# Own rows copied by ScalarE and fetched rows added by the gathering DMA, in a sparse graph kernel on one core

## The chip, the cores and the metric

The kernel runs on 1 core of one Trainium2 chip. The core has TensorE (PE, matrix products), VectorE (DVE), ScalarE (ACT), GpSimd (POOL) and SyncE (SP); each runs its own instructions in their order and waits for the others by semaphores. Data moves between HBM and the core's SBUF by 16 DMA engines. They are fed by queues: SP and ACT issue plain transfers (queues q1 and q10 in the profile), POOL issues transfers whose rows are named by an index list (q0). Time is device time from start to end of the one launch, in microseconds (us). The figure is the median of the runs; the profile is one more execution, with every instruction recorded.

## What is computed

The input is `x` of 32 matrices (512 nodes by 256 features) and one adjacency matrix `adj` of 512 x 512, about 1.6% of it and the diagonal not zero. Four graph layers follow each other. Layers 0 and 3 are the ones that matter here:

```python
pre_u = einsum('bud,dk->buk', h, W1[:d])
pre_v = einsum('bvd,dk->bvk', h, W1[d:])
hidden = relu(pre_u[:, :, None, :] + pre_v[:, None, :, :] + b1)
S = sigmoid(einsum('buvk,ko->buvo', hidden, W2)[..., 0] + b2[0])
a = einsum('buv,bud->bvd', S * A_a, h)
m = einsum('uv,bud->bvd', A_m, h) * h
z = beta1*h + beta2*(a @ Wa + ba) + beta3*(m @ Wm + bm)
```

For every pair of nodes (u, v) a row of 256 sums goes through a relu and is multiplied with `W2` and summed. `S` is multiplied with `adj`, so only pairs that `adj` holds count: these are the edges. Layer 1 is `z + relu(adj @ z @ W.T + b)`; layer 2 is an attention with a softmax over rows of 512.

## The kernel before

The kernel counts the nonzero entries at run time and takes a sparse path (`sparse_path`) when they fit, as they do here; the dense path is only compiled. In the sparse path, the 32 matrices go in 8 groups of 4 (`NB = 4`). For each group there are these streams of work, each a generator that yields after every piece:

- `first` loads `x`, turns it and computes `pre_u` and `pre_v` for all nodes (`pre`, lines 565 to 588). They are written by queue SP to a table in HBM with two rows of 1024 numbers per node: the even row holds `pre_u + b1` of the 4 matrices, the odd row `pre_v`.
- `edges` (lines 616 to 724), once for layer 0 and once for layer 3: the edge stage, which the change is in.
- `middle`: rest of layer 0, layers 1 and 2, and `pre` of layer 3. It starts by loading the matrix of `S * adj` (`load`, L732).
- `last`: the rest of layer 3.

An edge stage works through 36 items (`ITEMS`) of 128 edges each. An item has a tile `mine` [128 x 1024] with the `pre_u` rows of its 128 own nodes, and a tile `rows` [128 x 1024] with the `pre_v` rows of their neighbours. For 32 items the own nodes are a block of 128 consecutive nodes: `mine` is loaded by queue SP (L652) once for a block and used by 8 items. The last four items of the list are panels of left-over edges with own nodes of their own: there `mine` is gathered by POOL (L655). `rows` is gathered by POOL (`fetch`, L662, issuing at L612). There are 5 buffers for `rows` and 3 for `mine`.

Per item, VectorE adds the two tiles in place (L691). Then there are two ways to the relu, the product with `W2` and the sum over 256 features for each of 4 matrices. On even items, and on the last three, VectorE does it in four instructions, one for each matrix, that give the sum too (L707, `accum_out`). On odd items VectorE does relu and product in one instruction over 1024 columns (L699), and ScalarE makes the four sums (L677), issued one item later (`summed`). After every fourth item the sigmoid follows in small instructions (`exp_of`, L597 on ScalarE; `sigmoid_of` and `run_1`, L601, L602 and L641 on VectorE). Each item's 128 x 4 results are scattered by POOL into a matrix in HBM (`put`, L606), one `put` per item, in POOL's order between the gathers. A gather is called 3 items ahead of its use (`LEAD`).

Two of the 16 edge stages are run with little beside them: layer 0 of the first group and layer 3 of the last. They get `spare` buffers (`rows_more`, 8 in all) and a lead of 5, and there all items go by L699 and L677.

The order of the work is set by `weave`: every piece of every stream has a planned time (in units of one group), and pieces are issued in order of these times. The layer 0 edge stage of a group is planned to end 0.04 to 0.06 of a group before its middle begins. A scheduler then lays the instructions on each engine. `behind(ins)` (L499) keeps an edge instruction on its engine behind the last-but-one piece of the middle stage. Before the change it is used for the add (L691), the sums (L677) and small instructions, and not for the gathers.

Of the kernel before, what the change touches and what calls it, by code (L numbers as in the profile page):

```python
# [12 lines left out]
ALU = mybir.AluOpType  # L13
# [22 lines left out]
ITEMS = NC * OWN + 2 * PANELS  # L36
# [382 lines left out]
class Sparse:  # L419
# [94 lines left out]
    def setup(self):  # L514


        for w in (self.m.g0, self.m.g3):
            self.nc.vector.tensor_scalar(w["nb2"], w["b2"], -1.0, None, ALU.mult)
        self.zero = self.act.tile([P, GROUP], F32, name="zero", tag="hWa3")
        self.nc.gpsimd.memset(self.zero, 0.0)  # L520

        edges = self.built = self.e.build(self.counts, self.adjT, self.lists, self.psum, self.big, self.act)
        for _ in range(NC):
            next(edges)
            yield
        self.rest = self.m.rest(self.big(F32, 2048), self.psum)
        next(self.rest)
        self.zeros(self.cells["0"])
        yield
        for _ in range(NC + 2 * (OWN // 2 + 1)):  # L530
            next(edges)
            yield
# [74 lines left out]
            out=g.cells[half], out_offset=bass.IndirectOffsetOnAxis(ap=at, axis=0), in_=s, in_offset=None  # L607
        )

    def fetch(self, rows, g, at):  # L610

        self.nc.gpsimd.indirect_dma_start(  # L612
            out=rows, out_offset=None, in_=g.table, in_offset=bass.IndirectOffsetOnAxis(ap=at, axis=0)
        )

    def edges(self, g, spare=()):

        nc, e, w = self.nc, self.e, g.w  # L620
        flat = "p c b -> p (c b)"
        own = g.self_s.rearrange(flat)
        ready, fetched = [], {}
        lead = LEAD_AT_ENDS if spare else LEAD
        tags = [None] * 5 + list(spare)
        mine = {}
        places = g.table.rearrange("(c p k) n -> c k p n", p=P, k=2)

        def own_1():
            self.sigmoid_of(own)  # L630
            diag = self.counts.diag.unsqueeze(2).to_broadcast([P, NC, NB])
            nc.vector.tensor_tensor(g.self_s, g.self_s, diag, ALU.mult)
            for q in range(2):
                diagonal = g.cells[q][q * HALF : q * HALF + HALF * (N + 1), :]
                diagonal = diagonal.rearrange("(c p a) b -> p c a b", p=P, a=N + 1)[:, :, 0, :]
                nc.sync.dma_start(diagonal, g.self_s[:, 2 * q : 2 * q + 2, :])

        def run_1(ks):
            self.sigmoid_of(g.s[:, ks, :].rearrange(flat))
            value = e.value[:, ks].unsqueeze(2).to_broadcast([P, ks.stop - ks.start, NB])  # L640
            nc.vector.tensor_tensor(g.s[:, ks, :], g.s[:, ks, :], value, ALU.mult)  # L641
            for k in range(ks.start, ks.stop):
                j = e.order[k]
                ready.append((e.half_of(j), e.cell[:, j : j + 1], g.s[:, k, :]))

        def fetch(n):
            j = e.order[n]
            c = j // OWN
            if c >= NC or c not in mine:
                t = self.gath.tile([P, GROUP], F32, name="mine", bufs=3)  # L650
                if c < NC:
                    nc.sync.dma_start(t, places[c, 0])  # L652
                    mine[c] = t
                else:
                    self.fetch(t, g, e.iu[:, j - NC * OWN : j - NC * OWN + 1])  # L655
            else:
                t = mine[c]
            if tag := tags[n % len(tags)]:
                rows = self.act.tile([P, GROUP], F32, name="rows_more", tag=tag)
            else:  # L660
                rows = self.gath.tile([P, GROUP], F32, name="rows")
            self.fetch(rows, g, e.iv[:, j : j + 1])  # L662
            fetched[n] = rows, t

        def put():

            at = next((n for n, r in enumerate(ready) if r[0] != self.half), 0)
            if ready:
                r = ready.pop(at)
                self.half = r[0]  # L670
                self.put(g, *r)

        def sums(k, rows):

            for b in range(NB):
                part = rows[:, b * D : (b + 1) * D]
                self.behind(nc.scalar.activation(part, part, AF.Identity, accum_out=g.s[:, k, b : b + 1]))  # L677

        summed = []
        self.half = 1  # L680
        for n in range(lead):
            fetch(n)
            yield

        todo = [(2, lambda: self.exp_of(w, own)), (4, own_1)]
        done = 0
        for k in range(ITEMS):
            for _ in range(2 if spare and len(ready) > 2 else 1):
                put()
            rows, other = fetched.pop(k)  # L690
            self.behind(nc.vector.tensor_tensor(rows, rows, other, ALU.add))  # L691
            if k + lead < ITEMS:
                fetch(k + lead)
            if summed:
                summed.pop(0)()
            if spare or k % 2 == 1 and k < ITEMS - 3:
                by_entry = rows.rearrange("p (b d) -> p b d", b=NB)
                w2 = w["W2bc"].unsqueeze(1).to_broadcast([P, NB, D])
                nc.vector.scalar_tensor_tensor(by_entry, by_entry, 0.0, w2, ALU.max, ALU.mult)  # L699
                summed.append(lambda k=k, rows=rows: sums(k, rows))  # L700
                if spare:
                    summed.pop(0)()
            else:
                for b in range(NB):
                    part = rows[:, b * D : (b + 1) * D]
                    at = g.s[:, k, b : b + 1]
                    nc.vector.scalar_tensor_tensor(part, part, 0.0, w["W2bc"], ALU.max, ALU.mult, accum_out=at)  # L707
            if k % 4 == 3 or k >= ITEMS - 3:
                ks = slice(done, k + 1)
                near = spare or k >= ITEMS - 5  # L710
                todo.append((k + (1 if near else 3), lambda ks=ks: self.exp_of(w, g.s[:, ks, :].rearrange(flat))))
                todo.append((k + (1 if near else 4), lambda ks=ks: run_1(ks)))
                done = k + 1
            while todo and todo[0][0] <= k:
                todo.pop(0)[1]()
            yield
        for _, f in todo:
            f()
        for _ in range(TAIL - 1):
            put()  # L720
            yield
        while ready:
            put()
        yield
# [643 lines left out]
```

## Time and profile before

| | us |
|---|---|
| median of 3 runs | 3111.6 (3107.93 to 3116.17) |
| span of the profiled execution | 3112.8 |
| TensorE busy | 2713.5 (87%) |
| VectorE busy | 2302.9 (74%) |
| GpSimd busy | 1531.2 (49%) |
| ScalarE busy | 1337.7 (43%) |
| 16 DMA engines, mean busy share | 68% |

The profiled execution's own time is its span; it lies 1.2 us over the median. A line of the profile's groups reads: line of the kernel, engine, operation, destination <- sources, sizes and count, then busy us and mean ns of one, then the engine's idle us just before these instructions and what ended most of that. A table of waits reads: who waited, at which line, for whom, then us in total, times, longest. In a table of windows each row is a stretch of the span; for each engine it has busy us and number of instructions, then the granted TensorE clock, the busy share of the DMA engines and GB/s. Some records of a trace are missing: the page counts 552 gathers into `rows` and 24 into `rows_more`, which make up the 576, but other groups can be a few short.

### The profile page before, as it was taken

The numbers are of one execution on the slowest core, as the hardware profiler recorded it, in microseconds if no ns is written. First come the engines' busy times: TensorE is split into PE (matmuls) and PEld (weight loads), VectorE is DVE, ScalarE is ACT, GpSimd is POOL, SyncE is SP. The second block draws the span as 40 slices with busy tenths as digits, with TensorE's granted clock in tenths as the row PEclk, the third lists the DMA queues.
The fourth block names the chain that finished last, engine by engine and source line by source line (L and its number), as shares of the span: only waits on it lengthen the run. The fifth ranks groups of instructions, "written<-read, shape, count | busy, mean of one in ns | idle before, by whom it ended". The sixth has DMA issues, their size and how long they took to land. (4 is left out here: it accounts for less than half of the span.)

```text
span 3112.8 us, 32475 instructions
## 1 busy us (share of the span) xinstructions
PE 2713.5 (87%) x8645; PEld 1639.7 (53%) x8646; DVE 2302.9 (74%) x6027; ACT 1337.7 (43%) x4101; POOL 1531.2 (49%) x1328
## 2 busy tenths in 40 slices
PE   6367878889998899989998899989998899879957
PEld 3133444446654566446654565545654466546636
DVE  6964877888689776988489785888679795772761
ACT  3553454444344433444354442544345343443440
POOL 2561553656345552656346562555436563450461
PEclk9688889999999999999999999999999999999979
DMA  8774657776778757776678766787578766551753
GB/s 278 267 238 151 210 164 242 248 261 214 225 214 293 220 189 227 245 263 216 210 212 258 236 196 211 243 266 234 177 225 273 247 220 200 182 183 49 231 196 115
DMA packets 302719, 679.40 MB, mean 218 GB/s; under 512 B 52672, under 2 KB 170944, under 8 KB 294336
## 3 DMA queue, kind: packets, MB, share of 16 engines
q0 software_dynamic: 122688, 414.40, 42.6%
q1 hardware_dynamic: 160880, 225.62, 22.0%
q10 hardware_dynamic: 18960, 37.24, 3.2%
q8 instruction: 70, 1.15, 0.1%
q14 instruction: 121, 0.99, 0.1%
HBM read 531.12 MB, written 146.01 MB: 218 GB/s over the span
## 5 line engine op out<-in xcount | busy, mean ns | idle before, releaser
L606 POOL DMA_INDIRECT cells<-s,cell x576 | 686.4, 1192 | 747.0 <-DMA cells<-s,cell 388.5
L612 POOL DMA_INDIRECT rows<-table,iv x552 | 667.6, 1209 | 619.9 <-DMA table<-puv 150.5
L691 DVE TENSOR_TENSOR rows<-rows,mine 128x1024 f32<-128x1024 f32 x552 | 667.4, 1217 | 191.7 <-DMA rows<-table,iv 173.3
L677 ACT ACTIVATE rows<-rows 128x256 f32<-128x256 f32 x1088 | 439.8, 407 | 506.6 <-DVE rows L699 477.3
L45 PE MATMUL pst<-adj,h 128*128 128x512 f32 x1024 | 452.6, 594 | 0.3 <-PE pst L946 0.3
L707 DVE SCALAR_TENSOR_TENSOR rows<-rows,L_gnn_W2bc 128x256 f32<-128x256 f32 x1120 | 415.0, 417 | 1.8
L45 PE MATMUL pst<-L_gnn_Wa,hT 128*128 128x256 f32 x1024 | 261.3, 406 | 104.8 <-DMA hT<-xT 56.2
L699 DVE SCALAR_TENSOR_TENSOR rows<-rows,L_gnn_W2bc 128x1024 f32<-128x1024 f32 x272 | 329.7, 1214 | 0.3
L45 PEld LDWEIGHTS pst<-adj,h 128*128 128x128 f32 x1024 | 193.4, 191 | 223.3 <-issue 219.4
L45 PEld LDWEIGHTS pst<-L_gnn_Wa,hT 128*128 128x128 f32 x1024 | 204.8, 205 | 151.8 <-issue 85.1
L45 PE MATMUL pst<-eT,feats 128*128 128x512 f32 x512 | 230.9, 604 | 13.0 <-ACT eT L958 13.0
L866 PE MATMUL pst<-WT,hT 128*128 128x256 f32 x512 | 155.1, 470 | 96.0 <-DVE hT L853 96.0
L45 PE MATMUL pst<-adjT,zW 128*128 128x512 f32 x512 | 227.7, 597 | 3.8 <-ACT zW L870 3.8
L1006 PEld LDWEIGHTS pst<-hWa,SA 128*128 128x128 f32 x896 | 213.8, 328 | 7.7 <-issue 4.1
L1006 PE MATMUL pst<-hWa,SA 128*128 128x256 f32 x896 | 216.8, 398 | 0.0
L814 ACT COPY flat<-SA 128x512 f32<-128x512 f32 x128 | 137.7, 1127 | 165.9 <-PE pst L45 83.7
L677 ACT ACTIVATION_READ_ACCUMULATOR rows<-rows 128x1 f32 x1088 | 205.4, 189 | 0.0
L845 PE MATMUL pst<-flat,hWa 128*128 128x512 f32 x448 | 196.8, 592 | 0.0
L866 PEld LDWEIGHTS pst<-WT,hT 128*128 128x128 f32 x512 | 121.4, 242 | 136.6 <-DVE hT L853 107.1
L579 DVE TENSOR_TENSOR puv<-pst,bc_L_gnn_b 128x256 f32<-128x256 f32 x256 | 104.4, 414 | 95.8 <-DMA table<-puv 58.6
L580 ACT COPY puv<-pst 128x256 f32<-128x256 f32 x256 | 93.5, 370 | 180.6 <-DVE puv L579 162.7
L45 PEld LDWEIGHTS pst<-eT,feats 128*128 128x128 f32 x512 | 97.2, 193 | 127.5 <-issue 109.4
(172 smaller groups left out, 3984.4 us busy)
## 6 DMA issues: line engine op xcount, KB each, us to landing
table<-puv SPq DMA_DIRECT2D x256, 256.0 KB, 5.7
SA<-cells POOLq DMA_DIRECT2D x64, 1024.0 KB, 7.2
h<-in_x_dram SPq DMA_DIRECT2D x64, 512.0 KB, 6.5
mine<-table SPq DMA_DIRECT2D x64, 512.0 KB, 5.5
hT<-xT SPq DMA_DIRECT2D x36, 512.0 KB, 5.0
h<-x2s SPq DMA_DIRECT2D x36, 512.0 KB, 4.4
xT<-hT ACTq DMA_DIRECT2D x32, 512.0 KB, 6.1
x2T<-yT SPq DMA_DIRECT2D x32, 512.0 KB, 5.5
```

What stands on the lines that cost most here:

```text
L45: nc.tensor.matmul(out, lhsT, rhs, start=(n == 0), stop=(n == len(pairs) - 1))
L579: nc.vector.tensor_tensor(puv[:, 0, :], pp[:, 0:D], w["b1bc"], ALU.add)
L606: self.nc.gpsimd.indirect_dma_start(out=g.cells[half], out_offset=bass.IndirectOffsetOnAxis(ap=at, axis=0), in_=s, in_offset=None)
L612: self.nc.gpsimd.indirect_dma_start(out=rows, out_offset=None, in_=g.table, in_offset=bass.IndirectOffsetOnAxis(ap=at, axis=0))
L677: self.behind(nc.scalar.activation(part, part, AF.Identity, accum_out=g.s[:, k, b : b + 1]))
L691: self.behind(nc.vector.tensor_tensor(rows, rows, other, ALU.add))
L699: nc.vector.scalar_tensor_tensor(by_entry, by_entry, 0.0, w2, ALU.max, ALU.mult)
L707: nc.vector.scalar_tensor_tensor(part, part, 0.0, w["W2bc"], ALU.max, ALU.mult, accum_out=at)
L814: self.nc.scalar.copy(flat[:, r, :], SA[r][:, :, b])
L845: nc.tensor.matmul(pz, hWa[:, r, cs], flat[:, r, :], start=(r == 0), stop=False)
L866: nc.tensor.matmul(pw[:, at], zT[:, d, cs], m.WT_1[:, d, :], start=(d + k == 0), stop=(d * k == 1))
L1006: nc.tensor.matmul(pz[:, k * D : (k + 1) * D], SA[r][:, cs, b], hWa[:, r, :], start=(r + k == 0), stop=False)
```

## The change

The own rows are put into the `rows` tile first, by a ScalarE copy that is laid behind the middle stage. The gather then carries `compute_op=ALU.add`: the fetched rows are added to what the tile holds. VectorE's add (L691) goes. In the 14 stages that have work beside them VectorE now does all items in four instructions with sums; in the two spare stages odd items still go by the 1024-column instruction and ScalarE's sums, issued at once, and even items by VectorE alone. VectorE's instructions of these two kinds get `behind`, which the add had. The deferral of the sums (`summed`) is gone. Loads of `mine`, scatters, leads and numbers of buffers are as they were.

```diff
-    def fetch(self, rows, g, at):
+    def fetch(self, rows, g, at, **op):
         self.nc.gpsimd.indirect_dma_start(
-            out=rows, out_offset=None, in_=g.table, in_offset=bass.IndirectOffsetOnAxis(ap=at, axis=0)
+            out=rows, out_offset=None, in_=g.table, in_offset=bass.IndirectOffsetOnAxis(ap=at, axis=0), **op
         )
...
-            self.fetch(rows, g, e.iv[:, j : j + 1])
-            fetched[n] = rows, t
+            self.behind(nc.scalar.copy(rows, t))
+            self.fetch(rows, g, e.iv[:, j : j + 1], compute_op=ALU.add)
+            fetched[n] = rows
...
-            rows, other = fetched.pop(k)
-            self.behind(nc.vector.tensor_tensor(rows, rows, other, ALU.add))
+            rows = fetched.pop(k)
             if k + lead < ITEMS:
                 fetch(k + lead)
-            if summed:
-                summed.pop(0)()
-            if spare or k % 2 == 1 and k < ITEMS - 3:
+            if spare and k % 2 == 1:
                 by_entry = rows.rearrange("p (b d) -> p b d", b=NB)
                 w2 = w["W2bc"].unsqueeze(1).to_broadcast([P, NB, D])
-                nc.vector.scalar_tensor_tensor(by_entry, by_entry, 0.0, w2, ALU.max, ALU.mult)
-                summed.append(lambda k=k, rows=rows: sums(k, rows))
-                if spare:
-                    summed.pop(0)()
+                self.behind(nc.vector.scalar_tensor_tensor(by_entry, by_entry, 0.0, w2, ALU.max, ALU.mult))
+                sums(k, rows)
             else:
                 for b in range(NB):
                     part = rows[:, b * D : (b + 1) * D]
                     at = g.s[:, k, b : b + 1]
-                    nc.vector.scalar_tensor_tensor(part, part, 0.0, w["W2bc"], ALU.max, ALU.mult, accum_out=at)
+                    self.behind(
+                        nc.vector.scalar_tensor_tensor(part, part, 0.0, w["W2bc"], ALU.max, ALU.mult, accum_out=at)
+                    )
```

More of the change, by code (lines that the diff above doesn't have):

```diff
@@ L677, in sums @@
                 self.behind(nc.scalar.activation(part, part, AF.Identity, accum_out=g.s[:, k, b : b + 1]))
-        summed = []
         self.half = 1
```

## The prediction

> **What bounds the kernel now.** I read the page first: the span, the busy shares, the DMA queues, and the groups that the change touches.
>
> ```profile
> span 3112.8 us, 32475 instructions
> ...
> PE 2713.5 (87%) x8645; PEld 1639.7 (53%) x8646; DVE 2302.9 (74%) x6027; ACT 1337.7 (43%) x4101; POOL 1531.2 (49%) x1328
> ...
> q0 software_dynamic: 122688, 414.40, 42.6%
> q1 hardware_dynamic: 160880, 225.62, 22.0%
> ...
> L691 DVE TENSOR_TENSOR rows<-rows,mine 128x1024 f32<-128x1024 f32 x552 | 667.4, 1217 | 191.7 <-DMA rows<-table,iv 173.3
> L677 ACT ACTIVATE rows<-rows 128x256 f32<-128x256 f32 x1088 | 439.8, 407 | 506.6 <-DVE rows L699 477.3
> L699 DVE SCALAR_TENSOR_TENSOR rows<-rows,L_gnn_W2bc 128x1024 f32<-128x1024 f32 x272 | 329.7, 1214 | 0.3
> ```
>
> TensorE is busy 87% of the span, VectorE 74%, ScalarE 43%. The queue that carries the gathers (q0) keeps the 16 transfer engines occupied for 42.6% of the span; all queues together make 68%. The add that goes (L691) is VectorE's costliest group, 1.2 us a time. The span is 3112.8 us against a median of 3111.6, so I work against it directly.
>
> Averages hide stages, so I then cut the span into the opening, the long middle and the last edge stage.
>
> ```profile
> core 0: us, PE busy (x) PEld busy (x) DVE busy (x) ACT busy (x) POOL busy (x), PEclk, DMA share, GB/s
> ...
> 100.00:240.00 140.00, 77.64 (x196) 42.26 (x197) 109.24 (x223) 74.98 (x315) 85.39 (x70) 0.76 0.72 232
> ...
> 330.00:2890.00 2560.00, 2346.32 (x7486) 1404.52 (x7485) 1961.28 (x5311) 1115.95 (x3269) 1291.17 (x1105) 0.96 0.69 219
> 2890.00:3040.00 150.00, 105.89 (x354) 74.80 (x351) 105.08 (x143) 71.02 (x316) 90.58 (x72) 0.85 0.68 220
> ```
>
> In the middle, 82% of the span, TensorE works 2346 of 2560 us. It can give back at most 214 us there. The transfer engines stand at 0.69 of their time on average. In the opening and the last edge stage TensorE is busy only 55% and 71%: there the edge work itself sets the pace.
>
> What TensorE waits for in the middle comes from the table of waits (total us, times, longest):
>
> ```profile
> PE pst L866 <- DVE hT L853: 94.3, 21, 9.5
> PE pst L957 <- DVE ex L918: 41.0, 23, 8.3
> PE pst L957 <- DVE cols L917: 18.3, 3, 6.6
> ```
>
> These three, 154 us, all end with a VectorE instruction of the middle stage. So VectorE's queue is the main cause of what TensorE loses, and work taken from it can be worth something. POOL, which issues every gather and scatter in order, waits mostly for its own scatters to land:
>
> ```profile
> POOL cells L606 <- DMA cells<-s,cell: 346.3, 141, 6.3
> ```
>
> Last, how long a gather needs from issue to landing (min/median/max), and what the transfer engines do in a stretch that holds little but gathers and scatters:
>
> ```profile
> DMA to landing us min/median/max: 4.2/6.2/12.3
> ```
>
> ```profile
> 2980.00:3000.00 20.00, 9.27 (x24) 6.40 (x25) 14.72 (x18) 10.19 (x47) 16.10 (x12) 0.61 0.57 196
> ```
>
> **The change, part by part.**
>
> *VectorE.* Prices are the distance from one start to the next in VectorE's timeline.
>
> ```profile
> 1564.25 0.42 DVE L707 SCALAR_TENSOR_TENSOR rows<-rows,L_gnn_W2bc 128x256 f32<-128x256 f32 x1
> ...
> 1564.59 0.42 DVE L707 SCALAR_TENSOR_TENSOR rows<-rows,L_gnn_W2bc 128x256 f32<-128x256 f32 x1
> ...
> 1577.20 1.22 DVE L691 TENSOR_TENSOR rows<-rows,mine 128x1024 f32<-128x1024 f32 x1
> 1578.33 1.22 DVE L699 SCALAR_TENSOR_TENSOR rows<-rows,L_gnn_W2bc 128x1024 f32<-128x1024 f32 x1
> 1579.47 0.68 DVE L877 TENSOR_TENSOR yT<-yT,hT 128x512 f32<-128x512 f32 x1
> ```
>
> A quarter of a row tile with its sum takes 0.34 to 0.35 us, the add 1.13, a full-width multiply 1.14. The program has 576 adds; all go: 576 x 1.14 = 657 us. Full-width multiplies fall from 296 to 36: 260 x 1.14 = 296 us less. Quarters rise from 1120 to 2160: 1040 x 0.345 = 359 us more. Sum: 594 us less, from 2303 to 1709. On the path lies only the part behind the 154 us of TensorE waits above, and half of the VectorE work of the two end stages. Removing 26% of VectorE's work takes between 26% and all of the 154 us; I take half, 77 us. In the opening and the last stage each, 36 adds go (41 us), 18 full-width multiplies go (21 us) and 72 quarters come (25 us): 37 us less, of which half counts, together 37 us. The gain is bounded by 0 and 154 + 74 = 228 us; I take 114 us, if nothing else becomes late.
>
> *ScalarE.* It loses 1040 quarter sums of some 0.40 us (407 ns, and the 189 ns read of the accumulator overlaps the next): 421 us. It gains 576 copies of 128x1024. No such copy is in the trace. The 128x256 and 128x512 copies out of PSUM took 370 and 583 ns, which extends to 1.01 us; the 128x512 copy with strided input (L814) took 1127 ns, which doubles to 2.25. I take 1.2 us, nearer to the contiguous rows: the activations from SBUF of 256 and 512 columns (407 and 721 ns) extend to 1.35. That is 691 us; ScalarE goes to about 1608 us, 52%. This is hidden in its idle time as a sum (bounds 582 and 1296 us keep it under 72%), but not as a position, see below.
>
> *The gather with addition.* No accumulating transfer is in the trace. From below: the addition rides along with the bytes as they pass, and the gather costs what it costs now. From above: each row passes the engines three times instead of once (fetched, destination read, result written again), two extra passes. Between them: the destination's 512 KB must be read too, one extra pass of 512 KB. A pass is priced by the rows: 196 GB/s at a share of 0.57 is 344 GB/s at full share in the stretch above, and q1 moved 225.62 MB in 22.0% of the span, 329 GB/s. At 340 GB/s, 0.524 MB take 1.54 us of all 16 engines. I take one extra pass, because an addition into a tile cannot avoid reading that tile, and nothing shows that it must do more. For 504 gathers in the middle that is 776 us, a share of 0.30 on top of 0.69: 0.99. No stretch of 300 us in this trace holds more than 0.75, and only stretches of 20 us reach 1.0. So I let the engines sustain 0.95: the middle then takes 2560 x 0.99 / 0.95 = 2668 us, 108 us more. In the opening (100 to 240) the share of 0.72 is 101 us, with 36 x 1.54 = 55 us more 156, at 0.95 164 us: 24 us more. In the last stage 102 + 55 = 157, at 0.95 165: 15 us more. Together 147 us; by bounds 0 (no extra pass) to 2560 x (0.69 + 0.61) / 0.95 - 2560 = 943 us and some 80 us at the ends. Where transfers set the pace, VectorE's 114 us pay nothing.
>
> The Trainium skill has a rule for this, in "Collectives: The Full Stack", section "The bandwidth ceiling: the fold count and why AG ≠ RS ≠ AR": the addition in the transfer engine costs no cycles, but needs two source reads on the same ring, and so runs at half the rate of a copy. No run here shows an accumulating transfer yet. By that rule the gather's engine time doubles and the kernel ends as a forecast with one extra pass does; by the row of the plain gather alone it would end as the faster rival below.
>
> *The chain in front of a gather.* Until now the own rows ("mine", 5.5 us by queue SP, 6.0 by POOL) and the gather landed side by side. Now the own rows must have landed before the copy, the copy (1.2 us) before the gather is issued on POOL, and behind that gather POOL's queue holds the scatters, whose landing the matrices of the next middle stage wait for. Own rows are fetched at 8 of 36 items of a stage; the last four are panels, each with its own. A gather called three items ahead has 3 x 4.4 = 13 us (the 36 adds of one stage start between 1550 and 1707 us); mine 6.0 + copy 1.2 + issue 1.2 + landing 6.2 = 14.6 us, if every queue is free. The copies also stand in ScalarE's order ahead of zW and yT, which TensorE needs, and wait for VectorE to give up the buffer of five items before. Bounds: 0, if the lead covers it, to 7 us at each of 16 edge stages, 112 us. Only the eight of layer 0 stand directly in front of a middle stage, and the shortfall there is 2 to 4 us: I take 8 x 3 = 24 us. SP's queue is helped a little (the "mine" buffers come free at the copy), which I cost at nothing. TensorE's 7208 and SP's 621 rows in program order keep their number; POOL's 1362 too.
>
> Sum: 3113 + 147 + 24 = 3284; I say 3280 us.
>
> **The rivals.**
>
> *The addition is free and VectorE's relief comes through.* For it: TensorE's largest waits in the middle end with VectorE. Against it: the destination has to be read by something. 3113 - 114 = 3000 us, between 2890 and 3090. It decides if a gather keeps landing in some 6 us.
>
> *The transfers fit, but the longer chain eats the relief.* Share below 0.9, gathers at 6 to 7 us, POOL and ScalarE wait for each other: 3113 + 112 - 77 = 3148 us. For it speaks that POOL's in-order queue is already busy or waiting nearly always (1531 us busy, 346 us for scatters in the middle).
>
> *The addition is much dearer.* Two extra passes, or additions that do not pipeline: share 1.30 in the middle, 3113 + 943 + 80 = 4136 us at the bound; half way between one and two passes 3700 us. VectorE then waits for rows at nearly every item, and ScalarE's copies behind it. Nothing in the trace speaks against it, since it shows no such transfer.
>
> **How the numbers follow.** One extra pass 0.43, own range 3150 to 3450 (a sustained share of 1.0 to 0.9); free addition 0.27; chain only 0.12; much dearer 0.18. The range from 2990 leaves out 0.11 of the free case, up to 3700 leaves out half of the dear one, 0.09. A change of 0.3% (9 us) is about what a measurement of this kernel can tell. Faster: 0.27 and a little of the chain case, 0.29; same 0.04; slower 0.67.
>
> **What would show it.** VectorE busy near 1709 us and no L691; ScalarE near 1600 us with 576 copies of about 1.2 us. The share of q0 near 0.67 instead of 0.43 at the same bytes or more; landing of the gathers 8 to 10 us at the median. In VectorE's waits, rows from the gather well over the 145 us of the middle stage now; in POOL's, gathers that wait for ScalarE. I am wrong if the landing stays near 6 us and TensorE's waits for VectorE shrink (faster), or if the landing passes 15 us (much slower).

## The result, and the profile after

The changed kernel takes 3432.6 us (median of 4 runs, 3430.3 to 3440.4), beside 3113.9 us for the kernel before in the same comparison: the ratio is 1.1015, 95% interval [1.0986, 1.1044]. It is 319 us slower. The forecast was 3280 us with a range of 2990 to 3700: the direction and the main cause held, the loss is nearly twice as large as the forecast one.

The page of the profile after, with the lines that answer to those shown of before:

```profile
span 3438.6 us, 32511 instructions
...
PE 2795.5 (81%) x8645; PEld 1664.3 (48%) x8646; DVE 1759.5 (51%) x7271; ACT 1455.4 (42%) x2597; POOL 1681.4 (49%) x1328
...
q0 software_dynamic: 122688, 414.40, 58.5%
q1 hardware_dynamic: 160880, 225.62, 20.6%
...
HBM read 531.12 MB, written 146.01 MB: 197 GB/s over the span
...
L612 POOL DMA_INDIRECT rows<-table,iv x552 | 901.9, 1634 | 730.8 <-ACT rows L662 332.1
L703 DVE SCALAR_TENSOR_TENSOR rows<-rows,L_gnn_W2bc 128x256 f32<-128x256 f32 x2128 | 791.3, 419 | 804.8 <-DMA rows<-table,iv 801.7
L606 POOL DMA_INDIRECT cells<-s,cell x576 | 611.5, 1062 | 781.7 <-DMA cells<-s,cell 542.7
L662 ACT COPY rows<-mine 128x1024 f32<-128x1024 f32 x552 | 569.2, 1046 | 629.2 <-DVE rows L703 403.9
```

VectorE has lost 543 us of work (2302.9 to 1759.5), and TensorE is idle longer: 643 us of its span against 399. The gathers move the same 414.40 MB in as many packets, but q0 now occupies the engines for 58.5% of 3438.6 us, which is 2012 us, where it was 42.6% of 3112.8, 1326 us. By the page's count HBM traffic did not grow: 531.12 MB read and 146.01 MB written, as before. So what came on top in the transfer engines shows in their time and not in bytes from HBM. POOL needs 1634 ns to issue an adding gather, where a plain one had a mean of 1209 ns. ScalarE's copy takes 1046 ns. POOL's two groups read before:

```profile
L606 POOL DMA_INDIRECT cells<-s,cell x576 | 686.4, 1192 | 747.0 <-DMA cells<-s,cell 388.5
L612 POOL DMA_INDIRECT rows<-table,iv x552 | 667.6, 1209 | 619.9 <-DMA table<-puv 150.5
```

The windows of the same trace (a row is a stretch of the span: busy us and count by engine, granted TensorE clock, share of the DMA engines, GB/s) cover opening, middle and last edge stage, cut by eye at round numbers as those of before; each stretch came out longer:

```profile
core 0: us, PE busy (x) PEld busy (x) DVE busy (x) ACT busy (x) POOL busy (x), PEclk, DMA share, GB/s
100.00:260.00 160.00, 63.81 (x164) 35.81 (x163) 76.27 (x290) 70.95 (x209) 86.28 (x66) 0.68 0.85 186
330.00:3190.00 2860.00, 2458.32 (x7610) 1445.29 (x7609) 1519.62 (x6441) 1239.62 (x2036) 1433.61 (x1120) 0.94 0.84 200
3190.00:3360.00 170.00, 96.19 (x289) 66.56 (x287) 67.14 (x220) 70.52 (x199) 105.05 (x77) 0.79 0.86 191
```

The opening took 20 us more (160 for 140), the last edge stage 20 more (170 for 150), and the middle 300 more (2860 for 2560). Its DMA share rose from 0.69 to 0.84, and its GB/s fell from 219 to 200. The granted clock fell from 0.96 to 0.94. The three add up to 340 us where the span grew by 326, because the cuts do not fall on the same work (the middle holds 7610 matrix instructions here and 7486 before), so each is good to some ten or twenty us.

The table of waits for the whole trace (who waited, at which line, for whom: total us, times, longest) names the new waits:

```profile
DVE rows L703 <- DMA rows<-table,iv: 801.7, 317, 12.4
POOL cells L606 <- DMA cells<-s,cell: 542.7, 217, 8.3
...
PE pst L863 <- DVE hT L850: 112.4, 35, 10.0
```

VectorE waits 802 us for gathered rows, where its add waited 173. POOL waits 543 us for its scatters to land (before 388.5). TensorE waits 112 us for `hT` from VectorE (before 96). That row alone is little of what TensorE lost, but all of TensorE's rows in this table that end with VectorE add up to 393 us, before to 226, though VectorE has a quarter less to do. Its queue is in order, and it now stands at a row tile that has not landed while `hT` is behind it. One such place, in VectorE's timeline and then in TensorE's (start, us, instruction; in brackets the idle time before it and what ended it):

```profile
1527.86 0.42 DVE L703 SCALAR_TENSOR_TENSOR rows<-rows,L_gnn_W2bc 128x256 f32<-128x256 f32 x1 [6.34 <-DMA rows<-table,iv]
...
1532.12 0.42 DVE L703 SCALAR_TENSOR_TENSOR rows<-rows,L_gnn_W2bc 128x256 f32<-128x256 f32 x1 [2.61 <-DMA rows<-table,iv]
...
1533.51 0.69 DVE L850 TENSOR_TENSOR hT<-hT,pst 128x512 f32<-128x512 f32 x1
```

```profile
1534.25 5.83 PE L863 MATMUL pst<-WT,hT 128*128 128x256 f32 x16 [7.91 <-DVE hT L850]
```

VectorE stands 6.34 and 2.61 us at two row tiles, `hT` comes behind them, and TensorE waits 7.91 us for it.

### The profile page after: what moved, and what is told of

Same layout as the page of the kernel before. It is cut to its first block, busy times and chain, and to the rows that moved or that the text cites. A ratio compares the mean times of both kernels' runs of the same rounds, so it can differ in the third digit from the quotient of the medians.

```text
span 3438.6 us, 32511 instructions
## 1 busy us (share of the span) xinstructions
PE 2795.5 (81%) x8645; PEld 1664.3 (48%) x8646; DVE 1759.5 (51%) x7271; ACT 1455.4 (42%) x2597; POOL 1681.4 (49%) x1328
## 3 DMA queue, kind: packets, MB, share of 16 engines
q0 software_dynamic: 122688, 414.40, 58.5%
q10 hardware_dynamic: 18960, 37.24, 3.0%
HBM read 531.12 MB, written 146.01 MB: 197 GB/s over the span
## 5 line engine op out<-in xcount | busy, mean ns | idle before, releaser
L612 POOL DMA_INDIRECT rows<-table,iv x552 | 901.9, 1634 | 730.8 <-ACT rows L662 332.1
L703 DVE SCALAR_TENSOR_TENSOR rows<-rows,L_gnn_W2bc 128x256 f32<-128x256 f32 x2128 | 791.3, 419 | 804.8 <-DMA rows<-table,iv 801.7
L606 POOL DMA_INDIRECT cells<-s,cell x576 | 611.5, 1062 | 781.7 <-DMA cells<-s,cell 542.7
L662 ACT COPY rows<-mine 128x1024 f32<-128x1024 f32 x552 | 569.2, 1046 | 629.2 <-DVE rows L703 403.9
L45 PE MATMUL pst<-eT,feats 128*128 128x512 f32 x512 | 242.1, 628 | 29.3 <-ACT eT L955 28.3
L45 PE MATMUL pst<-adjT,zW 128*128 128x512 f32 x512 | 236.6, 617 | 18.0 <-ACT zW L867 18.0
L577 PE MATMUL pst<-w_L_gnn_W,yT 128*128 128x512 f32 x256 | 142.5, 685 | 58.0 <-DVE yT L932 56.7
L863 PEld LDWEIGHTS pst<-WT,hT 128*128 128x128 f32 x512 | 113.5, 229 | 156.7 <-DVE hT L850 132.1
L575 PE MATMUL pst<-w_L_gnn_W,hT 128*128 128x512 f32 x256 | 142.9, 686 | 55.8 <-ACT hT L562 52.5
L703 DVE DVE_READ_ACCUMULATOR rows<-rows,L_gnn_W2bc 128x1 f32 x2128 | 172.5, 81 | 0.0
```

The costliest lines, as they stand in the source:

```text
L45: nc.tensor.matmul(out, lhsT, rhs, start=(n == 0), stop=(n == len(pairs) - 1))
L575: nc.tensor.matmul(pp, hT[:, 0, ks], w["W1"][:, 0::DC, :], start=True, stop=False)
L577: nc.tensor.matmul(pp, hT[:, 1, cs], w["W1"][:, 1::DC, :], start=False, stop=True)
L606: self.nc.gpsimd.indirect_dma_start(out=g.cells[half], out_offset=bass.IndirectOffsetOnAxis(ap=at, axis=0), in_=s, in_offset=None)
L612: self.nc.gpsimd.indirect_dma_start(out=rows, out_offset=None, in_=g.table, in_offset=bass.IndirectOffsetOnAxis(ap=at, axis=0), **op)
L662: self.behind(nc.scalar.copy(rows, t))
```

## The experiments

The theory (A): the addition in the gather costs an extra pass in the transfer engines, and the time goes where those engines are occupied. Its rivals: (B) the longer chain in front of a gather (own rows, copy, gather) or too short a lead; (C) POOL's longer issue of the adding gather, in a queue that is in order; (D) the move of ScalarE's sums to VectorE.

### Plain gathers in place of adding ones

```diff
-            self.fetch(rows, g, e.iv[:, j : j + 1], compute_op=ALU.add)
+            self.fetch(rows, g, e.iv[:, j : j + 1])
```

> The changed kernel with the addition taken out of the gather: the copy by ScalarE stays in front of it, the gather is a plain one and overwrites what was copied, so the own rows are left out of the sum. If the addition's price on the transfer engines (or on POOL, which issues it) is the cause, the time falls to about 3000 to 3060 us, the share of the transfer engines returns to about 0.68 and VectorE's wait for gathered rows to under 200 us. If the chain own rows, copy, gather at a lead of three items is the cause, it stays at 3350 us or more.

3078.3 us (3074.0 to 3084.1), ratio to before 0.9871 [0.9819, 0.9923]. Engines' shares, two queues, POOL's issues, the middle by itself, and the waits of the whole trace:

```profile
PE 2706.9 (88%) x8646; PEld 1635.4 (53%) x8646; DVE 1752.5 (57%) x7271; ACT 1454.8 (47%) x2597; POOL 1326.8 (43%) x1328
...
q0 software_dynamic: 122688, 414.40, 42.1%
q1 hardware_dynamic: 160880, 225.62, 22.9%
...
L612 POOL DMA_INDIRECT rows<-table,iv x552 | 571.2, 1035 | 811.0 <-ACT rows L662 490.1
```

```profile
330.00:2860.00 2530.00, 2336.88 (x7500) 1397.46 (x7499) 1493.97 (x6356) 1220.56 (x2010) 1117.44 (x1106) 0.97 0.69 221
```

```profile
POOL rows L612 <- ACT rows L662: 490.1, 103, 100.7
DVE rows L703 <- DMA rows<-table,iv: 441.2, 206, 11.5
...
PE pst L863 <- DVE hT L850: 52.6, 11, 12.1
```

Copy, chain and order of issue are those of the changed kernel. POOL waits 490 us for ScalarE's copies, more than in the changed kernel (332), and still the kernel is faster than before. So with plain gathers the chain makes no such loss, and the addition, POOL's longer issue of it included, costs 3432.6 - 3078.3 = 354 us. This run also gives the worth of all of VectorE's relief, less whatever the chain costs: 1.3%, some 40 us. VectorE's wait for rows is 441 us here, 361 less, TensorE's wait for `hT` halves to 53 us, and all its waits that end with VectorE fall from 393 to 191 us. Time and wait both lie above what was expected (3000 to 3060 us, and under 200 us): VectorE's relief was worth less, and VectorE's wait for rows does not come back to the 173 us of before.

### What an adding gather costs by itself

A kernel with nothing but gathers of 128 x 1024 numbers, the same rows each time, in bursts of 30 into 5 tiles, and one after the other:

```python
for k in range(BURST):
    plain(rows[k % SLOTS])
clear()
for k in range(BURST):
    added(rows[k % SLOTS])   # the same, with compute_op=ALU.add
```

> A kernel that does nothing of the reference's work: it writes zeros to the output and then, twice, issues 8 plain gathers of 128 x 1024 one after the other, 8 with addition one after the other, 30 plain ones into five tiles and 30 with addition into five tiles. One extra pass: in the bursts 1.3 to 1.6 us a plain gather and 2.6 to 3.1 us one with addition. Free addition: the same for both. Two extra passes: 4 us and more. One after the other, an added gather lands 1 to 2 us later if the extra pass is all there is to it. POOL's issue takes 1.2 and 1.6 us, as in the traces of both kernels.

The groups of POOL's issues (line 51 is the adding, 48 the plain one), and two windows, in a burst of plain and in a burst of adding gathers:

```profile
L51 POOL DMA_INDIRECT r<-in_x_dram,at x76 | 117.5, 1546 | 144.0 <-DVE spot L61 75.7 <-DMA r<-in_x_dram,at 42.6 <-DVE at L45 22.0
L48 POOL DMA_INDIRECT r<-in_x_dram,at x76 | 71.6, 942 | 131.6 <-DVE spot L57 75.1 <-DVE at L45 31.3 <-DMA r<-in_x_dram,at 16.6
```

```profile
core 0: us, DVE busy (x) POOL busy (x), PEclk, DMA share, GB/s
356.00:388.00 32.00, 0.00 (x0) 23.41 (x25) 1.00 1.02 393
186.00:240.00 54.00, 0.00 (x0) 33.84 (x22) 1.00 1.06 211
```

The engines are occupied wholly in both (shares of 1.02 and 1.06), but move 393 GB/s plain and 211 GB/s adding. From one gather's start to the next in the bursts it is 1.28 us plain and 2.48 us adding, so the addition is worth 1.20 us of all 16 engines for 512 KB, a little below the expected price of one extra pass and far from that of two. POOL's first issues of a burst, which wait for no landing, stand 1.24 us apart plain and 1.85 adding, so the plain burst is near POOL's limit as well as the engines', while the adding one is held by the engines. The issue on POOL takes 1546 ns for 942, 0.60 us more. One after the other, the distance is 5.1 us plain (in the second round, when nothing else moves) and 6.9 us adding.

The Trainium skill states in "Collectives: The Full Stack", section "The bandwidth ceiling: the fold count and why AG ≠ RS ≠ AR", that in a ring of four ranks ReduceScatter, which adds, runs at half the rate of AllGather, which copies, because the add needs two source reads on the same ring (62.28 against 32.35 GB/s there). The runs here, which are no ring of ranks, give the same ratio for a gather into SBUF with all 16 engines: 2.48 to 1.28 us is a factor of 1.94.

### An extra plain pass instead of the addition

With plain gathers, one further transfer of 512 KB per gather, from a resident tile to a scratch tensor in HBM. First on SyncE's queue:

```diff
+            nc.sync.dma_start(self.dump[self.dumped % 8], self.m.adj[:, 0:2, :].rearrange("p c d -> p (c d)"))
```

> The kernel after the change with the addition taken out of the gather (own rows missing in the sums, as in the run with plain gathers), and with one extra plain transfer of 512 KB per gather on SyncE's queue, from a resident tile in SBUF to a scratch tensor that nobody reads. In the run with the two kinds of gathers alone, the addition cost 1.20 us of the engines per 512 KB; the extra transfer should cost some 1.2 to 1.5 us. GpSimd's issue stays as short as with plain gathers. If the time of the transfer engines makes the loss, this kernel stands near the kernel after: 3350 to 3450, with a share of the transfer engines of about 0.84 in the middle. If GpSimd's longer issue makes it, it stays at 3080 to 3120 although the share rises. SyncE's other transfers stand behind the extra ones in its queue, which may add something of its own.

3416.0 us, ratio 1.0963 [1.0912, 1.1015]. The time is that of theory A, but the run isn't as clean as meant: nothing tied these transfers to the gathers, and SyncE had issued all of them by about the middle of the program. Its queue, and two windows, one in each half:

```profile
q1 hardware_dynamic: 243824, 527.65, 42.5%
```

```profile
900.00:1200.00 300.00, 240.25 (x726) 141.38 (x726) 146.50 (x609) 118.02 (x200) 102.70 (x102) 0.90 1.00 372
2400.00:2700.00 300.00, 281.47 (x920) 173.84 (x919) 175.86 (x753) 138.10 (x220) 140.38 (x140) 0.97 0.70 223
```

The extra time on q1 is 42.5% of 3422.0 us less 22.9% of 3082.4, 748 us, and the kernel is 338 us longer than with plain gathers: 0.45 us per microsecond, although the engines stood near 1.00 for that half of the program. To have the passes at the pace of the gathers, the transfer was put on ScalarE's queue, directly behind the copy of its item:

```diff
-            self.behind(nc.scalar.copy(rows, t))
+            copy = nc.scalar.copy(rows, t)
+            self.behind(copy)
+            self.dumped += 1
+            extra = nc.scalar.dma_start(self.dump[self.dumped % 8], self.m.adj[:, 0:2, :].rearrange("p c d -> p (c d)"))
+            order = mybir.DependencyInfo(mybir.DependencyClass.NoSync, mybir.DependencyReason.DATA)
+            self.tc.add_manual_dep(extra.ins, copy.ins.name, order, reason="behind the copy")
             self.fetch(rows, g, e.iv[:, j : j + 1])
```

> As the run with one extra plain transfer of 512 KB per gather (no addition, own rows missing in the sums), but the transfer is issued on ScalarE's queue directly behind ScalarE's copy of the item, so that the extra passes come at the pace of the gathers; in the earlier run SyncE had issued all of them in the first half of the program. Without extra transfers 3078, with the addition 3433. If the engines' time makes most of the loss also when it is spread evenly (a share of 0.69 + 0.25 in the middle if nothing slowed down): 3280 to 3450. If evenly spread passes fit into the engines' idle time, and the loss of the addition is GpSimd's issue (3183 with it alone) and the gather's own latency: 3080 to 3180.

3488.8 us, ratio 1.1184 [1.1140, 1.1228]. That is above the expected 3280 to 3450. Its queues, the landing of the extra transfers, and most of the middle (q10 is ScalarE's, which held 37.24 MB and 3.2% before):

```profile
q0 software_dynamic: 122688, 414.40, 35.5%
q10 hardware_dynamic: 101904, 339.26, 25.2%
...
dump<-adj ACTq DMA_DIRECT2D x576, 512.0 KB, 7.4
```

```profile
330.00:2900.00 2570.00, 2168.20 (x6677) 1280.19 (x6676) 1374.46 (x5900) 1116.68 (x1829) 1027.74 (x1032) 0.92 0.86 298
```

And the control: the same issue and waits, but 4 KB moved in place of 512.

```diff
-            extra = nc.scalar.dma_start(self.dump[self.dumped % 8], self.m.adj[:, 0:2, :].rearrange("p c d -> p (c d)"))
+            extra = nc.scalar.dma_start(self.dump[self.dumped % 8], self.m.adj[:, 0, 0:8])
```

> The kernel with the evenly spread extra transfer per gather (plain gathers, own rows missing in the sums), with the extra transfer cut from 512 KB to 4 KB (128 x 8 numbers): the same issues in ScalarE's queue, the same waits on the scratch tensors, but next to nothing moved. Without any extra transfer 3078, with 512 KB each 3489. If the time of the transfer engines made those 411 us, this kernel comes back to 3080 to 3140. If the issues on ScalarE's queue made a good part of them, it stays above 3200, and that part has to be taken off what the extra pass is said to cost.

3127.4 us, ratio 1.0025 [1.0004, 1.0047].

```profile
q0 software_dynamic: 122688, 414.40, 42.2%
...
q10 hardware_dynamic: 101904, 39.63, 4.7%
```

```profile
330.00:2900.00 2570.00, 2340.76 (x7481) 1396.51 (x7480) 1491.67 (x6342) 1224.41 (x2005) 1115.34 (x1107) 0.96 0.70 219
```

Of the 411 us (3489 - 3078), 49 come with the issues, the waits and the small packets on ScalarE's queue, and 361 with the bytes. These bytes occupied the engines for 25.2% of 3495.9 less 4.7% of 3126.0, 734 us. Each microsecond of extra engine time, spread at the pace of the gathers, made the kernel 0.49 us longer. The addition put 2012 - 1298 = 714 us on q0 (1298 is 42.1% of 3082.4, with plain gathers). At 0.49 this is 351 us; measured are 354. That the two agree so closely is partly a matter of counting: while q10 gained 734 us, q0 and q1 together gave back some 75, so that all queues gained 658 us, which makes 0.55 and an estimate of 392 us for the addition. Either way theory A accounts for the loss without anything else. The pass is a stand-in and not the same transfer: it writes 302 MB to HBM, which the addition does not. Part of how it acts is latency: in the paced run a gather lands 7.5 us after its issue at the median, with plain gathers alone after 5.7. The runs do not separate the time for which the engines are occupied from the later landing that goes with it.

### POOL's longer issue

With plain gathers, a GpSimd copy in front of each, so that its queue gets as much as the adding gather costs it:

```diff
+            pad = self.gath.tile([P, N], F32, name="pad", bufs=1)
+            nc.gpsimd.tensor_copy(pad, rows[:, 0:N])
             self.fetch(rows, g, e.iv[:, j : j + 1])
```

> The kernel after the change with the addition taken out of the gather (own rows are copied, but then overwritten by the plain gather, so they are missing in the sums, as in the run with plain gathers), and with a GpSimd copy of 128x512 put in front of every gather. That copy took 626 ns in the trace of before, so GpSimd's in-order queue gets about the 0.61 us per gather that the adding gather costs it, and the transfer engines get nothing more. The same kernel without that copy took 3078 us, with the addition 3433. If GpSimd's longer issue of the adding gather makes the loss, this kernel loses most of the 354 us too: 3250 to 3430. If the time of the transfer engines makes it, this one stays at 3080 to 3110. In between, the share of the way is GpSimd's part.

3182.8 us, ratio 1.0215 [1.0165, 1.0265]: 105 us over the run with plain gathers, 30% of the addition's loss, between the two cases expected. The busy row, and the groups of VectorE's quarters and of the added copy:

```profile
PE 2742.1 (86%) x8645; PEld 1644.0 (52%) x8646; DVE 1943.0 (61%) x7271; ACT 1461.2 (46%) x2597; POOL 1727.7 (54%) x1904
```

```profile
L705 DVE SCALAR_TENSOR_TENSOR rows<-rows,L_gnn_W2bc 128x256 f32<-128x256 f32 x2128 | 928.6, 483 | 488.6 <-DMA rows<-table,iv 467.7 <-POOL pad L664 16.2 <-issue 4.2
L664 POOL COPY pad<-rows 128x512 f32<-128x512 f32 x552 | 383.3, 694 | 542.2 <-ACT rows L662 535.1 <-DVE rows L705 3.4 <-DVE cols L916 1.1
```

The stand-in is too strong in two ways. POOL's busy time rose by 401 us (1326.8 to 1727.7), where the addition raised it by 355. And VectorE became slower: a quarter takes 483 ns in the mean instead of 420 (the median is 418, the longest took 1302), and VectorE is busy 1943 us for the same work that took 1752.5. The adding gather did no such thing (419 ns). So POOL's part is probably below 105 us; it is not separated from VectorE's slowing.

Both stand-ins together, the paced pass and the copy on POOL:

> The same kernel with both stand-ins for the addition: the evenly spread extra transfer of 512 KB per gather, and the GpSimd copy of 128x512 in front of the gather (own rows missing in the sums). If occupied engines and GpSimd's longer issue together are the whole of the addition's loss, this comes to the time of the kernel after, 3390 to 3480. If it stays clearly below 3390, something else of the adding gather costs too, first of all its own latency from issue to landing, which neither stand-in lengthens by itself.

3591.4 us, ratio 1.1526 [1.1481, 1.1571]. They add up (411 + 105 = 516 over 3078; measured 513) and go well beyond the changed kernel and the expected 3390 to 3480, so no further cost of the adding gather has to be assumed. How the 354 us divide between engine time and POOL's issue stays open in so far as the two stand-ins exceed it together: engine time alone explains it, and a part of up to some 100 us for POOL isn't excluded.

### A longer lead

Gathers called four items ahead, with a sixth row tile, for which one of the three tiles of own rows was given up:

```diff
-LEAD = 3
+LEAD = 4
...
-        self.act, self.small, self.gath = pool("act", 1), pool("small", 2), pool("gath", 5)
+        self.act, self.small, self.gath = pool("act", 1), pool("small", 2), pool("gath", 6)
...
-                t = self.gath.tile([P, GROUP], F32, name="mine", bufs=3)
+                t = self.gath.tile([P, GROUP], F32, name="mine", bufs=2)
```

> The changed kernel with one more buffer for rows (6, paid with one of the three for own rows) and a lead of 4 instead of 3. If the transfer engines' time is the limit, the time stays within 1% of 3433 us. If the longer chain is what is late, four items cover it better and the time falls to 3250 to 3330 us.

3625.0 us, ratio 1.1621 [1.1558, 1.1684], slower than the changed kernel, which neither case of the expectation allowed. Two things were changed at once, so the lead was tried alone, with 5 row tiles and 3 of own rows:

> The kernel after the change with gathers called four items ahead in the middle stages in place of three, and nothing else; the run with four ahead, a sixth row tile and one tile fewer for the own rows took 3625. If the missing tile for the own rows made that run slow, and the latency of the adding gather is part of the loss, a longer lead helps: 3300 to 3400. If the loss is occupied engines, lead changes nothing: within 1% of 3433. If the longer lead itself bunches the gathers or keeps row tiles from being free, it is slower: 3500 and more.

3454.0 us, ratio 1.1105 [1.1049, 1.1160]: within 1% of the changed kernel. In the waits, first of the run with two tiles for own rows, then of the run with the lead alone:

```profile
ACT rows L662 <- DMA mine<-table,iu: 607.0, 56, 14.8
```

```profile
ACT rows L662 <- DVE rows L703: 482.8, 192, 16.9
...
ACT rows L662 <- DMA mine<-table,iu: 123.9, 20, 16.3
```

With two tiles for own rows ScalarE's copy waits 607 us for the own rows of the panels; with three, 124. So the missing tile is what made that run slow, as far as the waits tell. The lead by itself is no help. With five row tiles the copy of the fourth item ahead waits for the tile that VectorE has just left (483 us against 404 with a lead of three), so this run doesn't tell what a longer lead with more tiles would give; six row tiles beside three for own rows were not run.

### Half of the gathers with addition

The kernel before, with copy and addition on even items of the 14 stages (and the last three), odd items as before: 280 of 576 gathers add.

```diff
+        def added(n):
+            return not spare and (n % 2 == 0 or n >= ITEMS - 3)
...
+            op = {}
+            if added(n):
+                self.behind(nc.scalar.copy(rows, t))
+                op["compute_op"] = ALU.add
+            self.fetch(rows, g, e.iv[:, j : j + 1], **op)
```

> The kernel before with the change made for half of the items: in the middle stages, ScalarE's copy and the adding gather for even items (and the last three), whose quarters VectorE sums; odd items as before (plain gather, VectorE's addition, ScalarE's sums); the end stages as before. 280 of 576 gathers add. If every adding gather costs the same, whatever stands beside it, the time lies half way: about 3270. If the loss only begins when transfers stand above some share of the engines' time, half of the extra 1.2 us per item (a share of 0.69 + 0.13 in the middle) is largely hidden: 3110 to 3150.

3326.1 us, ratio 1.0681 [1.0625, 1.0736]. Neither case expected this much. Its q0 and most of its middle:

```profile
q0 software_dynamic: 122688, 414.40, 51.3%
```

```profile
330.00:2900.00 2570.00, 2225.62 (x6948) 1319.60 (x6947) 1578.83 (x4750) 1279.38 (x3334) 1316.88 (x1052) 0.94 0.79 208
```

q0 has 51.3% of 3328.7 us, 382 us more than before, and the kernel is 209 us longer: 0.55 us per microsecond of engine time. So the loss does not wait for a share above 0.79: there it is present already, and with 66% of the whole change's 319 us it is more than half. That the rest of VectorE's relief is missing here may be why; no run shows it.

### The second half of the change alone, and its opposite

The kernel before, with VectorE taking the sums of all items in the 14 stages, and of the even items in the two spare ones:

```diff
-            if spare or k % 2 == 1 and k < ITEMS - 3:
+            if spare and k % 2 == 1:
```

> The kernel before with only the second half of the change: VectorE makes the sums that ScalarE made, the add stays with VectorE. VectorE's work rises by 224 x 0.25 us plus 36 x 0.25, some 65 us, to about 2370 us. If that half matters by itself, the time rises by 1 to 2%, to 3140 to 3180 us; if VectorE's spare time takes it, it stays within 0.5% of 3113 us.

3139.3 us, ratio 1.0071 [1.0044, 1.0099]. This half costs 0.7% by itself (theory D: it loses, but little). That suggested the opposite as a version better than both: all items but the last three by VectorE's full-width multiply and ScalarE's sums.

```diff
-            if spare or k % 2 == 1 and k < ITEMS - 3:
+            if spare or k < ITEMS - 3:
```

> The kernel before (VectorE adds, plain gathers), with ScalarE taking the sums of all items but the last three in the middle stages, in place of every second item: 238 more items go by one full-width multiply on VectorE (1.14 us in place of four quarters of 0.345) and four sums on ScalarE. VectorE has some 57 us less, ScalarE some 390 us more. The opposite step, all sums on VectorE, took 0.7% longer than before. If that loss came from VectorE's load, this kernel gains as much: ratio 0.990 to 0.997. If ScalarE's order of work becomes the new wait (the sums stand ahead of what TensorE needs), it loses: 1.005 to 1.03.

3184.2 us, ratio 1.0219 [1.0175, 1.0263]: it loses, as in the second case expected. Busy row and TensorE's waits, and POOL's wait for ScalarE's sums:

```profile
PE 2724.6 (85%) x8645; PEld 1643.8 (51%) x8646; DVE 2253.1 (70%) x4361; ACT 1714.1 (54%) x6005; POOL 1562.4 (49%) x1328
```

```profile
PE pst L866 <- DVE hT L853: 120.8, 26, 14.3
PE pst L957 <- DVE ex L918: 67.5, 31, 11.2
```

```profile
POOL rows L612 <- ACT rows L677: 326.4, 124, 32.7
```

VectorE is relieved by 50 us, and TensorE waits longer for it all the same: 121 us for `hT` and 68 for `ex`, before 96 and 41. All its waits that end with VectorE add up to 270 us, before to 226: they do not follow VectorE's busy time. What grew is POOL's wait for ScalarE to be done with a row tile before the next gather into it, 326 us where it was 70, and VectorE's wait for rows, 228 us for 173. Of the three splits tried, the one of before is the best; no version beat it with the whole computation done.

## Why the prediction was right in sign and short in size

- **The extra pass.** Right in kind: one pass, not none and not two. Predicted 1.54 us of all engines, from 340 GB/s; measured 1.20 us by itself and 714 / 576 = 1.24 us in the kernel. The share of q0 was forecast at 0.67 and is 0.585, partly because the pass is cheaper and partly because the span is longer.
- **"So I let the engines sustain 0.95."** This is the step that failed. It let extra engine time fill the idle 0.31 of the middle up to 0.95 and charged only the rest, 108 us. In the kernel the middle went from 2530 us (plain gathers) to 2860, some 330 us by these windows, and the share stood at 0.84. With the measured pass of 1.24 us the same step would have given 504 x 1.24 = 625 us, a share of 0.69 + 0.24 = 0.93, and so nothing at all. The engines can be occupied more: the pass that wasn't tied to the gathers held 1.00 over 300 us. But that pass was paid as well. About half of every added microsecond of engine time comes back as time, whether the engines stand at 0.79 (0.55, half of the gathers adding), at 0.84 to 0.86 (0.49 to 0.55, all adding or the paced pass) or near 1.00 for half of the program (0.45). The path on which it acts is seen: gathers land later (7.5 us for 5.7 with the paced pass), VectorE stands at their rows, and TensorE waits for what is behind them in VectorE's queue (393 us for 191 with plain gathers). Why it comes to about half was not tested.
- **The ends.** Predicted +24 and +15 us; measured some +20 to +30 (POOL issues the last gather of the opening's edge stage at 240 us, before at 209) and +20.
- **VectorE's relief, 114 us "if nothing else becomes late".** Too large: the run with plain gathers, which has all of it and the longer chain too, gains 40 us over before, where 114 less the chain's 24 would have been 90. The sum of the work was near (1709 forecast, 1759.5 measured: a quarter with its accumulator read holds VectorE 0.45 us in the mean, by busy time, where 0.345 was taken from a row of quarters close behind each other). "Half of the 154 us" was a guess on TensorE's waits for VectorE, and these are decided by VectorE's order: its waits for rows stand ahead of `hT`. In the sum, the relief was set to nothing where transfers set the pace, so this error did not enter the forecast; it made the rival of 3000 us too low. Even with an addition for nothing the kernel would have come to 3078.
- **ScalarE.** Copy 1.2 us forecast, 1.046 measured; in all 1608 forecast, 1455 measured. As a sum it is hidden, as forecast; in its order less so: TensorE's waits that end with ScalarE went from 57 to 105 us (73 with plain gathers).
- **The chain, 24 us.** Not seen as a loss: with it and with plain gathers the kernel is faster than before, and a lead of four, with five row tiles, changes nothing. What it cost against the relief can't be told apart.
- **What was missed.** POOL's issue of an adding gather takes 0.60 us more, 355 us of POOL's time between the two kernels; the prediction left POOL's issues at their price. Its part in the loss is between nothing and some 100 us.
- **What would show it.** VectorE's rows waits well over 145 us: 802. POOL's gathers waiting for ScalarE: 332 us, but more (490) in the run that is faster, so this sign told nothing. The landing times of 8 to 10 us can't be read: the traces of kernels with adding gathers give none. The prediction's counts 7208, 621 and 1362 stand in no page; the pages have 8645 matrix instructions and 1328 of POOL in both kernels, so that the numbers stay the same holds for these two.

The step "an addition into a tile cannot avoid reading that tile" held, but that the sign came out right is partly luck. With the pass at its measured 1.24 us, the prediction's own sum would have charged nothing for the middle and some 17 us for the ends, which makes 3154 us with the chain. And since a share of 0.93 lies below the 0.95, half of VectorE's 154 us would have counted too, which ends near 3080 us, faster than before. A pass priced too high made up for a step that let the engines' idle time take it for nothing.

## What to carry to other kernels

An addition in a gather moves work from VectorE to the transfer engines at 1.2 us for 512 KB, where VectorE's own add took 1.13 us; that pays only where the transfers are not part of the loop that sets the pace. When transfers wait for results and results for transfers, don't fill the engines' idle share first and charge the rest: here about half of every extra microsecond of engine time came back as time, at mean shares of 0.79 and above. And what taking work off an engine is worth is read from what stands in its queue ahead of the awaited instruction, not from its busy time.

## What the runs showed of the hardware

- An adding gather has 1.94 times the engine time of a plain one (2.48 against 1.28 us for 512 KB), and 0.60 us more issue on POOL, while the bytes read from HBM stay the same (531.12 MB).
- POOL's issues became shorter when VectorE's 128x1024 instructions went: a plain gather took 1209 ns in the mean before, and 1035 ns with plain gathers after; a scatter 1192 and 1049. With the adds left and nearly all of VectorE's full-width multiplies gone (the split alone) they took 1160 and 1169. And a GpSimd copy lengthened VectorE's quarters from 420 to 483 ns in the mean. The Trainium skill, in "SBUF — State Buffer", section "🔬 SBUF: two separate sides", says that the two engines share a pair of ports, locked for a whole instruction, also when VectorE has two SBUF inputs and GpSimd reads SBUF; these quarters have two. For the copy the direction agrees; no run here isolates the lock, and what lengthens the issues was not tested.
- TensorE's granted clock went with its idleness: 0.946 at 88% busy (plain gathers), 0.942 (before), 0.916 at 81% (after), 0.904 at 80% (paced pass). The same products took 2707, 2714, 2796 and 2800 us. Of the 326 us by which the span grew, 82 are busy time of TensorE. That the waits lower the clock, and so cost a second time, fits these numbers but was not tested.
